# Layer 0's mixer in a fixed order by phase, with its closing norm kept in PSUM and its first state written by ScalarE

## The chip, the cores and the metric

The kernel runs on one core of a Trainium2 chip. The metric is device time in microseconds (us) of one execution; the number of record is the median of several runs. Five engines work side by side, each through its own queue in program order: PE (TensorE, matrix products; PEld is its loading of weights), DVE (VectorE), ACT (ScalarE), POOL (GpSimd) and SP (here only the issuing of transfers). They wait for each other by semaphores. Matrix products land in PSUM, which has eight banks of 128 x 512 fp32; everything else lies in SBUF.

## The reference, cut to what matters

The whole program is four layers on an image of 4 x 32 x 128 x 128 fp32. Only layer 0 is touched. For each of the four images (`b`), with 32 time steps of 128 nodes x 128 features, it computes a group norm, a graph attention with a layer norm after it, and then a selective state-space mixer (Mamba) over the 32 time steps, whose result is normed and added to the input:

```python
xz = xt @ in_proj                       # xc (256 wide) and the gate z (256 wide)
xc = silu(conv over 4 time steps of xc)
dbc = xc @ x_proj                       # dt's input, B (16), C (16)
dt = softplus(dbc[..., :8] @ dt_w + dt_b)
def step(hprev, inp):                   # for each of 32 time steps
    dA_t, dBx_t, C_t = inp              # dA = exp(-dt*exp(A_log)), dBx = dt*xc*B
    hnew = dA_t * hprev + dBx_t         # state: 128 nodes x 256 channels x 16
    return hnew, einsum('bds,bs->bd', hnew, C_t)
y = (ys + Dp * xc) * silu(z)
out = y @ out_w + out_b                 # then h + out, layer norm (gain nt_g, bias nt_b), x + that
```

## The kernel before

`layer0` (a function of class `Kernel`) goes through the four images. Each image has two stages: `gat`, the attention, in 8 groups of 4 time steps; and `mamba`, the mixer, in 8 blocks of 4 time steps. Both write no instruction directly. They register **parts** (an engine, a cost in us, a function that issues some instructions, what it comes after, which buffers it takes and frees) with a planner, class `Parts`; `emit` then orders all parts by a list schedule: of the parts that could start, it takes the one that starts first by the costs, ties within a `patience` going to the lower **rank** (a number per kind, `RANKS`, plus the part's place in time). Every engine then executes its instructions in just the order of emission (`in_order`). The costs, the stretch factors and the ranks are thus all that decides the order in each queue.

What a mixer block does, by the names that the prediction uses:

- `mamba_block` prepares a block while the block before it runs: `conv` (8 matmuls of 512 columns into two banks), `xsilu` (ACT, Silu), `xproj`, `dbc`, `dtproj`, then softplus by `dabs`, `dexp`, `one`, `dln` (Ln), `back` on ACT, `relu` on DVE and `dplus` (L1060) and `dsub` (L1063) on POOL, which ends in `dt`; `xturn` and `umul` (L1074, DVE) make `u` = dt x xc, `bct` and `bc` (L1085) B and C.
- `mamba_gates` makes silu(z): two matmuls (`gatep`) into two banks, then both banks by ACT (`zsilu`).
- `step` does one time step in four quarters of four states each. Per quarter: `decay` (POOL, L755) makes dt x A into `e` (three buffers); `expo` (ACT, L761) puts exp(-e) into a PSUM pair `pa` (two such pairs); `mul` (DVE, L775) multiplies by the state `S` in place; `plus` (DVE, L783, four instructions) adds u x B and writes `S`. For the fourth quarter ACT makes u x B (`ub`, L791) and one DVE sum adds it (L795). The first time step has no old state: DVE writes u x B straight into `S` (L785, 16 instructions from SBUF to SBUF). `diagp` (POOL, L772) and `diag` (ACT, L767) make diagonals of C, and `read` (PE, L808) contracts S with them into the PSUM tile `yp`; `fetch` (ACT, L816) copies that out, `turn` (PE, L821, L826) turns it and adds Dp x xc, and `gate` (DVE, L834) multiplies by silu(z).
- `output` closes the block: `project` (PE, L876 to L882, one part) into a bank of the pool `pm`; `ofetch` (ACT, L888) copies the bank to SBUF, which frees it; `stats` (DVE, L895, L897), `power` (POOL, L901 to L904), `norm` (ACT, L909) and `sums` (POOL, L913, L914, L916: times gain, plus bias, plus X).

PSUM is divided into `pa` (four banks), `yp` (two) and `pm` (two banks, for everything else; a part that takes a `pm` bank has to come after the one that frees it). ACT holds one table of functions at a time; a change among Exp, Silu and Ln puts a table load in front. When block 6 is registered (`HEAD`), parts of the next image's attention are registered too, named `ahead`: `gat_open` makes its coefficients (DVE L398 to L403, then PE's spread L407, then ACT's copy L411), and `gat_inputs` the inputs of its first two groups. The rank `EARLIER` puts them late in the order. The last block's close of images 0 to 2 is left to the next image's `gat`.

## Time and profile before

| what | us |
|---|---|
| runs of the kernel, median (lowest to highest of 3) | 3815.86 (3815.35 to 3816.46) |
| the profiled execution, its own time | 3811.59 |
| its span, from the first to the last instruction | 3809.8 |
| mean granted TensorE clock | 0.88 |
| layer 0 | 0 to about 2283 |
| the mixers, from first decay (L755) to last read-out (L816) | 162 to 595, 723 to 1158, 1286 to 1718, 1844 to 2267 |
| the three attention stages between them | 128, 128, 126 |

Busy shares over the span are PE 82%, DVE 77%, ACT 70%, POOL 66%; but they are a mean over four layers with different limits, and POOL has little to do after layer 0. The page's line of POOL in 40 slices shows this:

```profile
POOL 3699896699996799896799980133456522067940
```

Each digit is a slice of 95 us, 9 for 90% and more. The four runs of 8 and 9 up to slice 24 are the four mixers. The profile's groups name an instruction by its line in the kernel, its engine, and what it writes and reads; "idle before" is the time that its engine stood still just ahead of it, with the instruction that ended this.

### The profile page before, as it was taken

The page shows a single profiled execution, that of the slowest core. Times are in us where ns is not written, and L with a number is a line of the kernel's source. Part 1 is how long each engine was busy: PE and PEld are TensorE (multiplying, and loading weights), DVE is VectorE, ACT ScalarE, POOL GpSimd, SP SyncE. Part 2 cuts the span into 40 slices and gives each one's busy share as a digit, 9 for nine tenths or more (in the row PEclk, how much of TensorE's full clock was granted, in tenths as well). Part 3 has the DMA queues.
Part 4 walks back from the last instruction along what each step waited for, and adds up shares of the span by engine and source line. Part 5 has one row for each costly group of instructions (what it writes and reads, how often), then busy time and mean ns, then how long its engine had stood idle before and what let it go on. Part 6 is the DMA issues. An engine that isn't in the chain of part 4 may idle for free. (4 is left out here: it accounts for less than half of the span.)

```text
span 3809.8 us, 64520 instructions
## 1 busy us (share of the span) xinstructions
PE 3133.8 (82%) x23495; PEld 2082.4 (55%) x23495; DVE 2938.7 (77%) x6986; ACT 2676.5 (70%) x5577; POOL 2525.0 (66%) x2043
## 2 busy tenths in 40 slices
PE   7888888888878888778888868787868987988877
PEld 4555455455545454455445447665547753587655
DVE  6788997898997898897789875577869856386942
ACT  5799896789896888886899873334566654176753
POOL 3699896699996799896799980133456522067940
PEclk8888899988999988899888885797869998998989
DMA  3000000000000000000000000000002000700003
GB/s 127 1 1 1 1 1 1 1 1 1 1 1 1 1 1 1 1 1 1 1 1 1 1 12 7 1 1 1 1 18 81 1 1 3 267 4 1 1 1 89
DMA packets 51654, 61.38 MB, mean 16 GB/s; under 512 B 5850, under 2 KB 31140, under 8 KB 51204
## 3 DMA queue, kind: packets, MB, share of 16 engines
q1 hardware_dynamic: 36740, 42.12, 3.3%
q10 hardware_dynamic: 14592, 15.08, 1.1%
q8 instruction: 188, 3.08, 0.3%
q14 instruction: 134, 1.10, 0.1%
HBM read 48.80 MB, written 8.39 MB: 15 GB/s over the span
## 5 line engine op out<-in xcount | busy, mean ns | idle before, releaser
L755 POOL TENSOR_TENSOR e<-dt,Ar 128x1024 f32<-128x1024 f32 x496 | 1180.1, 2412 | 33.4 <-ACT pa L761 32.2
L775 DVE TENSOR_TENSOR pa<-pa,S 128x1024 f32<-128x1024 f32 x496 | 607.0, 1224 | 49.6 <-ACT pa L761 48.7
L783 DVE SCALAR_TENSOR_TENSOR S<-u,BC,pa 128x256 f32<-128x256 f32 x1488 | 615.3, 475 | 22.8 <-DVE pa L775 1.4
L761 ACT ACTIVATE pa<-e 128x1024 f32<-128x1024 f32 x496 | 502.7, 1019 | 83.1 <-DVE S L783 37.6
L808 PE MATMUL yp<-S,Dp 64*64 64x256 f32 x4096 | 359.0, 504 | 122.3 <-issue 57.4
L808 PE MATMUL yp<-S,D 64*64 64x256 f32 x4096 | 293.9, 397 | 93.3 <-DVE S L795 69.7
L808 PEld LDWEIGHTS yp<-S,Dp 64*64 64x64 f32 x4096 | 192.8, 175 | 274.2 <-issue 155.9
L767 ACT ACTIVATE D<-I,BC 128x64 f32<-128x64 f32 x1024 | 262.5, 337 | 0.1
L808 PEld LDWEIGHTS yp<-S,D 64*64 64x64 f32 x4096 | 155.5, 138 | 185.4 <-issue 63.0
L1006 PE MATMUL pm<-h,Wm 128*128 128x512 f32 x512 | 237.0, 612 | 0.0
L826 PE MATMUL pm<-I,y 128*128 128x64 f32 x1024 | 171.9, 299 | 55.9 <-ACT y L816 55.9
L791 ACT ACTIVATE ub<-u,BC 128x256 f32<-128x256 f32 x496 | 210.1, 495 | 9.6 <-DVE S L795 6.8
L559 POOL TENSOR_TENSOR e<-e,den 128x512 f32<-128x512 f32 x128 | 131.7, 1041 | 118.6 <-DVE den L555 69.3
L772 POOL TENSOR_TENSOR Dp<-I,BC 128x256 f32<-128x256 f32 x256 | 156.2, 626 | 78.9 <-PE yp L808 70.5
L826 PEld LDWEIGHTS pm<-I,y 128*128 128x128 f32 x1024 | 162.1, 226 | 63.8 <-ACT y L816 63.8
L547 ACT ACTIVATE e<-sc,mn 128x128 f32<-128x128 f32 x512 | 145.9, 400 | 31.9 <-DVE mn L542 19.1
L1006 PEld LDWEIGHTS pm<-h,Wm 128*128 128x128 f32 x512 | 95.7, 194 | 116.4 <-issue 115.7
L795 DVE TENSOR_TENSOR S<-pa,ub 128x1024 f32<-128x1024 f32 x124 | 151.6, 1222 | 6.0
L821 PE MATMUL pm<-xc,DD 128*128 128x128 f32 x512 | 129.0, 338 | 5.3 <-DVE dt L1045 5.3
L542 DVE TENSOR_REDUCE mn<-sc 128x4 f32<-128x512 f32 x128 | 83.0, 680 | 57.3 <-PE sc L533 41.4
L821 PEld LDWEIGHTS pm<-xc,DD 128*128 128x128 f32 x512 | 88.8, 217 | 48.2 <-issue 37.1
L761 ACT ACT_TABLE_LOAD x88 | 112.9, 1283 | 1.5
(599 smaller groups left out, 8093.1 us busy)
## 6 DMA issues: line engine op xcount, KB each, us to landing
w<-in_L_ffn_weight_dram SPq DMA_DIRECT2D x22, 1024.0 KB, 14.7
w<-in_L_ffn_weight_dram ACTq DMA_DIRECT2D x10, 1024.0 KB, 13.7
out_dram<-o ACTq DMA_DIRECT2D x16, 256.0 KB, 2.9
out_dram<-o SPq DMA_DIRECT2D x16, 256.0 KB, 2.9
X<-in_x_dram SPq DMA_DIRECT2D x4, 512.0 KB, 5.6
A<-in_L_conv_A_log_dram SPq DMA_DIRECT2D x1, 2048.0 KB
cw<-in_L_conv_conv_w_dram SPq DMA_DIRECT2D x1, 512.0 KB
sh<-in_sh_dram SPq DMA_DIRECT2D x1, 512.0 KB, 3.7
```

Source lines behind the costliest of these rows:

```text
L755: nc.gpsimd.tensor_tensor(v["e", q], node("dt").unsqueeze(1).to_broadcast([P, 4, 256]), Ar[:, 4 * q : 4 * q + 4, :], ALU.mult)
L761: nc.scalar.activation(v["a", q], v.pop(("e", q)), AF.Exp, scale=-1.0)
L767: nc.scalar.activation(v["D", q][:, r, :], I2, AF.Copy, scale=g["BC"][:, i, s : s + 1])
L772: nc.gpsimd.tensor_tensor(v["D", q], I2.unsqueeze(1).to_broadcast([P, 4, 64]), C, ALU.mult)
L775: nc.vector.tensor_tensor(v["a", q], v["a", q], S[:, 4 * q : 4 * q + 4, :], ALU.mult)
L783: nc.vector.scalar_tensor_tensor(S[:, s, :], node("u"), Bt, a[:, r, :], ALU.mult, ALU.add)
L791: nc.scalar.activation(v["b", q][:, r, :], node("u"), AF.Copy, scale=g["BC"][:, i, s : s + 1])
L795: nc.vector.tensor_tensor(S4, v.pop(("a", q)), v.pop(("b", q)), ALU.add)
L808: nc.tensor.matmul(v["y"][o : o + 64, n, :256], D[ns, r, :], S[ns, s, :], start=(s < 2), stop=(s >= 14), skip_group_check=True,)
L821: nc.tensor.matmul(v["p"][:, j * P : (j + 1) * P], DD[:, j, :], g["xc"][:, j, cs], start=True, stop=False)
L826: nc.tensor.matmul(v["p"][:, o : o + 64], v["y"][:, n, j * P : (j + 1) * P], I2, start=False, stop=(n == 1))
L1006: nc.tensor.matmul(g["x", j], Wm[:, i, j * P : (j + 1) * P], rows(4 * k + 3 - i), start=(i == 0), stop=(i == 3))
```

## The change

The mixer's planner no longer makes a list schedule. Each part gets the rank `block x PERIOD + phase`, where `PERIOD` is 52.093 and `PHASES` holds one phase for each part of a block by its kind, and `emit` issues the parts in order of rank, each as soon as all that it comes after has been issued. All blocks have so the same order. The parts `ahead` have ranks of block 0 to 3. Beside this:

- `output`: `project` in four parts; no `ofetch`; `stats` and `norm` work on the bank itself; the product with the gain (`gain`) is DVE's, in the bank; the bias is added to X by POOL (`shift`), at any time before; `total` (DVE) adds bank and X. The bank is held until `total`. Where the next image's attention closes the last block (images 0 to 2), the copy and the three sums stay.
- `plus` of the first time step is 16 ACT copies with a scale instead of 16 DVE instructions.
- `mamba_gates` and `mamba_block` take one bank at a time for each half (`zsilu`, `xsilu`), and `conv` is eight parts of one matmul.
- Costs of most kinds, the stretch factors and the ranks of `gat` (still list-scheduled, with an added 0.13 us between dependent parts of one engine) have new values.

The diff, cut to its core (new values of costs and of the tables left out):

```diff
+    def emit(self):
+        if self.by_rank:
+            left = sorted(self.parts, key=lambda p: p["rank"])
+            while left:
+                p = left.pop(next(i for i, p in enumerate(left) if self.start(p) is not None))
+                for h in p["take"]:
+                    self.taken[h["name"]].append(h)
+                p["end"] = 0.0
+                p["fn"]()
+            return
...
-        plan = Parts(latency=0.25, window=300, patience=self.PATIENCE, stretch=Parts.STRETCH)
-        hold, pace = plan.hold, 25.5
-        def add(kind, at, *args, **kwargs):
-            plan.rank = at * pace + self.RANKS[kind]
+        plan = Parts()
+        plan.by_rank, seen = True, {}
+        hold = plan.hold
+        def add(kind, k, *args, **kwargs):
+            n = seen[kind, k] = seen.get((kind, k), -1) + 1
+            plan.rank = k * self.PERIOD + self.PHASES[kind][n]
             return plan.add(*args, **kwargs)
...
-                        nc.vector.tensor_scalar(S[:, s, :], node("u"), Bt, None, ALU.mult)
+                        nc.scalar.activation(S[:, s, :], node("u"), AF.Copy, scale=Bt)
...
+            def take():
+                g["x"] = g.pop("p").rearrange("p (a f) -> p a f", f=F)
+                stats()
+            def shift():
+                nc.gpsimd.tensor_tensor(xs, xs, ntb.unsqueeze(1).to_broadcast([P, 4, P]), ALU.add)
+            def gain():
+                nc.vector.tensor_tensor(g["x"], g["x"], ntg.unsqueeze(1).to_broadcast([P, 4, P]), ALU.mult)
+            def total():
+                nc.vector.tensor_tensor(xs, g["x"], xs, ALU.add)
...
-            p = add("project", 4 * k + 4, PE, 3.4, project, g["gates"], [hx, hp], [g["h"]["yg"]])
-            p = add("ofetch", 4 * k + 4, ACT, 0.52, fetch, [p], (), [hp])
+            for i in range(4):
+                p = add(
+                    "project", k, PE, 1.6 if i == 0 else 0.78, lambda i=i: project(i), [p] if i else g["gates"],
+                    () if i else [hp], [g["h"]["yg"]],
+                )
...
+                p = add("stats", k, DVE, 1.06, take, [p])
+                p = add("power", k, POOL, 1.78, power, [p])
+                p = add("norm", k, ACT, 1.54, norm, [p])
+                p = add("gain", k, DVE, 0.6, gain, [p])
+                x = add("shift", k, POOL, 1.23, shift)
+                add("total", k, DVE, 0.6, total, [p, x], (), [hp])
...
                 def ahead(kind, at, *args, **kwargs):
-                    plan.rank = self.EARLIER * pace + at
-                    return plan.add(*args, **kwargs)
+                    return add("ahead", 0, *args, **kwargs)
...
-        hs, c = [hold("pm", 2), hold("pm", 2)], None
+        c, p = None, None
         for j in range(2):
-            c = add("gatep", 4 * k, PE, 0.92, lambda j=j: gatep(j), [c], () if j else [h["sz"], *hs])
-        g["sz ready"] = [add("zsilu", 4 * k, ACT, 1.0, both, [c], (), hs, "silu")]
+            hp = hold("pm", 2)
+            c = add("gatep", k, PE, 0.965, lambda j=j: gatep(j), [c], [hp] if j else [h["sz"], hp])
+            p = add("zsilu", k, ACT, 0.49, lambda j=j: zsilu(j), [c, p], (), [hp], "silu")
+        g["sz ready"] = [p]
```

In the order of the changed program's instructions (it has no times in it) a block runs on POOL with one `shift` and no `sums`, on DVE from `stats` to `total` as: stats, L783's four, L775, L783's four, L775, `gain`, L795, `total`, and on PE from `project` to the first matmul of conv's second half as: six quarters of `read` with conv's first four matmuls between them. The coefficients of the next image stand on DVE ahead of the stage's first L775, and the `ahead` copy of ACT ahead of the last four copies of the first state. The program has 142 table loads, 60 fewer than before; 58 POOL instructions fewer and 58 DVE products more; 64 DVE scalings fewer and 64 ACT copies more; 29 ACT bank copies fewer.

## The prediction

> **What bounds the kernel now.** I read the busy time by stage first, then the groups, then who waited for whom inside a stage, then single stretches of the timeline. Layer 0 handles four images in turn; each has an attention stage (some 128 us) and a mixer stage (some 430 us). Busy time of PE, PEld, DVE, ACT and POOL in the second image's mixer, the third's attention and the fourth's mixer, then clock and DMA:
>
> ```profile
> 723.00:1158.00 435.00, 355.37 (x2945) 215.40 (x2944) 395.42 (x668) 378.44 (x694) 398.99 (x245) 0.87 0.00 1
> 1158.00:1286.00 128.00, 109.22 (x990) 68.56 (x982) 90.13 (x233) 92.38 (x237) 79.54 (x97) 0.97 0.01 1
> 1844.00:2267.00 423.00, 349.69 (x2913) 213.71 (x2914) 377.20 (x658) 377.11 (x696) 393.47 (x242) 0.86 0.00 1
> ```
>
> In a mixer stage POOL is busy 399 of 435 us, DVE 395, ACT 378: POOL leads, two others are close behind. The big groups (out<-in, count, busy, mean ns):
>
> ```profile
> L755 POOL TENSOR_TENSOR e<-dt,Ar 128x1024 f32<-128x1024 f32 x496 | 1180.1, 2412 | 33.4 <-ACT pa L761 32.2
> L775 DVE TENSOR_TENSOR pa<-pa,S 128x1024 f32<-128x1024 f32 x496 | 607.0, 1224 | 49.6 <-ACT pa L761 48.7
> L783 DVE SCALAR_TENSOR_TENSOR S<-u,BC,pa 128x256 f32<-128x256 f32 x1488 | 615.3, 475 | 22.8 <-DVE pa L775 1.4
> L761 ACT ACT_TABLE_LOAD x88 | 112.9, 1283 | 1.5
> ```
>
> Durations overlap a little, so I price by starts of neighbours. POOL's timeline in a mixer, and the end of a block in it:
>
> ```profile
> 788.16 14.23 POOL L755 TENSOR_TENSOR e<-dt,Ar 128x1024 f32<-128x1024 f32 x6
> ...
> 817.21 1.21 POOL L772 TENSOR_TENSOR Dp<-I,BC 128x256 f32<-128x256 f32 x2
> 818.35 2.37 POOL L1060 TENSOR_TENSOR dt<-dt,u 128x1024 f32<-128x1024 f32 x1
> 820.80 2.36 POOL L1063 TENSOR_TENSOR dt<-dt,u 128x1024 f32<-128x1024 f32 x1
> 823.24 2.39 POOL L755 TENSOR_TENSOR e<-dt,Ar 128x1024 f32<-128x1024 f32 x1
> ```
>
> ```profile
> 516.14 1.30 POOL L913 TENSOR_TENSOR xn<-xn,ntg 128x512 f32<-128x512 f32 x1
> 517.51 1.28 POOL L914 TENSOR_TENSOR xn<-xn,ntb 128x512 f32<-128x512 f32 x1
> 518.87 1.27 POOL L916 TENSOR_TENSOR X<-X,xn 128x512 f32<-128x512 f32 x1
> 520.10 2.39 POOL L755 TENSOR_TENSOR e<-dt,Ar 128x1024 f32<-128x1024 f32 x1
> ```
>
> One block of the mixer on POOL: 16 decays of 14.23/6 = 2.37 make 37.9; four pairs of diagonals of 1.14 (817.21 to 818.35) 4.6; dplus and dsub 4.9 (818.35 to 823.24); the norm's power step 1.8 (L901 at 808.34 to the next decay at 810.12); the three sums 4.0 (516.14 to 520.10). Together 53.1 us. By POOL's timeline the blocks 1 to 7 of the last image begin 55.1 us apart on average (1883.7 to 2214.3, six periods), those of the second 55.9 (770.1 to 1105.6). So POOL is idle 2.0 us a block, 2.8 where the next image's inputs are opened in the same stage. **A mixer block is POOL's own work plus two to three us.**
>
> Two stretches show something else. DVE builds the first state (L785), then next image's coefficients (L398), while POOL runs:
>
> ```profile
> 720.42 16.97 DVE L785 TENSOR_SCALAR S<-u,BC 128x256 f32<-128x256 f32 x16
> ```
>
> ```profile
> 429.07 9.32 POOL L755 TENSOR_TENSOR e<-dt,Ar 128x1024 f32<-128x1024 f32 x4
> ...
> 431.31 7.10 DVE L398 TENSOR_TENSOR gc<-gd 128x1 f32<-128x1 f32 x1
> ```
>
> L785 takes 0.34 us where POOL rests and up to 2.5 us beside a decay; 16 of them fill 17.0 us. L398, a 128x1 product, ends at 438.41, just as POOL's four decays end (438.39). The same line takes 0.16 us at 19.9 us, where POOL has little to do. Both read SBUF alone; DVE's other large groups read a bank as well and show no such stretch.
>
> **The change, part by part.**
>
> *Closing norm in its bank.* For 29 of 32 blocks POOL's three sums become one (shift): -2 x 1.35 = -2.7 us, so 53.1 becomes 50.4. DVE gains two products of 128x512 with one side in a bank. Nearest rows: half of L775's 1.13 us between starts, and L591 (0.58 to 0.62); I take 0.6 each, +1.2. ACT loses the copy L888 (0.48). DVE's block by starts: 16 x 1.13 (L775) + 12 quarters x 4 x 0.39 (L783) + 4 x 1.13 (L795) + 3.9 (gates, relu, umul, BC) + stats 1.04 + 1.2 = 47.6, plus 0.13 for each L775 whose own L783 follows at once (median of its starts 1.26 against 1.13), some 1.2: 48.8. Still under POOL's 50.4. The trace of before has no stats or norm on a bank that is also the matmul's target; bounds: stats between 0.19 (L596, SBUF) and 0.17 a quarter (0.69/4, L355 from a bank), so nothing either way.
>
> [...]
>
> *Tables.* The changed program holds 142 table loads where before has 202. 60 x 1.29 us (start to next start) = 78 us less on ACT, about 2.4 a block. ACT is not the bound, so this is worth nothing alone; it is the cover for the first state, and it shortens the wait of L775 on ACT (48.7 us in all).
>
> *First state by ACT.* 64 L785 leave DVE (14.9, 17.0, 15.0 and 9.3 us in the four stages) and 64 copies of 128x256 come to ACT, 0.40 each by L791: 6.4 us a stage.
>
> *Ahead.* The next image's coefficients move from the middle of the stage (block 4) to its head. In before they come with a POOL idle of 2.8 - 2.0 = 0.8 us a block, 4.8 us a stage, in three stages; that goes. But in the changed order the product that was L398 stands behind POOL's power of the next image, and POOL has 2 decays and 3 diagonals (2 x 2.37 + 3 x 0.57 = 6.5 us) right behind that. I take the full 6.5 us, by the 7.10 row. Behind it on DVE stand the diagonals; behind these, PE's spread, which holds the first reads; behind the spread ACT's copy of the row, and behind that the last quarter of the first state, a diagonal, a table load and the first exponential: 15.8 us after dsub for the row (dsub, powers and the first decay 7.5, stall 6.5, diagonals and PE 1.8), +1.6 +1.0 +1.3 +1.0 = 20.7 to the first L775. Before it is 21.3, 22.4 and 20.5 (dsub's end 714.9 to 737.3). So the head gains nothing in three stages; in the fourth, without that product, 14.3 against 14.0.
>
> [...]
>
> *Order by phases.* Every block follows one fixed order instead of a list made by due times. After the first exponential ACT has, in the new order, 12 exponentials (0.95), two diagonals or inputs between most of them, four table loads and the next block's chain: 40 us to block 1, against 36.4 from the first L775 now: +3 a stage. The next block's conv to dsub stands at fixed places, and POOL's last decay of a block comes well before dplus, so POOL must wait when that chain is late. I keep the idle at 2.0 a block: 50.4 + 2.0 = 52.4. Bounds: 1.0 (the waits of POOL on PE, 18.4 us of the second mixer, mostly gone) and 4.0 (twice). The last block: 52.8 us from its first decay to its last read-out; fewer sums, but POOL now ahead of DVE: -1.
>
> *Gates by bank, conv in single matmuls, project in four:* the same instructions on PE and ACT, in smaller parts. PE is busy 355 of 435 us and hides them: nothing; without that cover a late bank costs what the held-bank rival below prices. *Attention ranks:* two table loads fewer (2.6 us of ACT beside PE's 109 of 128), other order unknown, bounds -5 and +5: I take -2 a stage.
>
> **Sum.** Mixers of images 1 to 3: 6 x (55.9 - 52.4) = 21, +1, -3 = 19 each, 57. Fourth: 6 x (55.1 - 52.4) = 16, +1, -3 = 14. Attention 4 x 2 = 8. End of the layer, where the sums are bare: copy 0.5 and 2.7 gone, 3. Total 82. The profiled execution took 3811.59 us (span 3809.8); less 82, 3729.6. The median of the runs is 3815.86, 4.3 above: **3734 us**.
>
> **Rivals.**
>
> *DVE becomes the bound.* 48.8 plus its waits: in the second mixer 32 us (13.5 on umul's bank, 11.4 on ACT, 4.9 on gates, others 2.2), 4 a block; 48.8 + 4.0 = 52.8, and with somewhat more in a fixed order 53.7: 28 blocks x 1.3 = 36, **3770**. For it: DVE gains 1.2 a block where POOL loses. Against: table loads caused part of the waits.
>
> *More than forecast.* No stall at the head (-5 x 3), idle of 1.5 (-0.5 x 28): **3705**; with attention at -5, 3693.
>
> *The held bank stalls PE: slower.* A project bank was free after 0.6 us of copy; now it is held through stats, power, norm, gain and total, one of two. In the new order PE has 6 quarters of reads (1.09 each by L808's 16 records) and 4 conv matmuls (0.93 each) before conv's second half wants that bank: 10.2 us. DVE's order from stats to total is 1.0 + 5.4 + 0.6 + 1.1 + 0.6 = 8.8 if power (1.8) and norm (1.5) return within the 5.4. They have 1.8 us to spare there and 1.4 at PE; a decay (2.4) ahead of power and an input group (1.6) ahead of norm eat 4.0. Beyond 3.2 us, conv is late, then dplus, and POOL idles by as much. At 4 us a block: 28 x 4 = 112, **3846**; it decides from 82/28 = 2.9 us a block. Against: only both queues at their worst give 0.8.
>
> *Nothing to be seen:* a fixed order loses just what POOL saves, 3816. That the change does not do what it says I rule out: its program has 58 fewer POOL instructions and 60 fewer loads.
>
> **Chances.** Forecast 0.45 (own range 3710 to 3755), DVE 0.25, more 0.15, held bank 0.12, nothing 0.03. Faster by over 0.2% 0.85, within 0.2% (about what a measurement can tell from no change) 0.03, slower 0.12. With the bounds of idle (1.0: -28; 4.0: +56) and attention (-12, +28) the range is 3680 to 3800.
>
> **What would show it.** Blocks 1 to 7 begin 52.4 us apart on POOL; shift once a block; the old L398 takes some 6 us in three stages, and POOL idles at the head for it; mixer stages of 413 to 416 us, the fourth 409; L775's wait on ACT below 40. Wrong if POOL's idle per block is above 3, if conv waits for total, or if DVE's waits fall on gain.

## The result, and the profile after

| | before | changed |
|---|---|---|
| runs: median (lowest to highest), us | 3815.98 (3815.34 to 3819.27, 6 runs) | 3842.05 (3829.98 to 3862.76, 6 runs) |
| ratio, 95% interval | | 1.0072 (1.0045 to 1.0099) |
| profiled execution, span | 3809.8 | 3837.3 |
| mean granted clock | 0.880 | 0.881 |

The change made the kernel 0.7% slower; 3734 was forecast. The stages of the changed kernel, second image's mixer, third's attention, fourth's mixer (columns as in the prediction: busy us of PE, PEld, DVE, ACT, POOL, then the granted clock):

```profile
718.60:1170.10 451.50, 372.21 (x2950) 226.42 (x2950) 384.51 (x672) 365.60 (x696) 389.70 (x242) 0.85 0.00 1
1170.10:1294.90 124.80, 106.30 (x978) 67.31 (x978) 87.72 (x224) 87.27 (x229) 71.79 (x86) 0.97 0.01 1
1859.20:2295.40 436.20, 362.44 (x2915) 218.61 (x2916) 375.29 (x663) 363.59 (x692) 385.34 (x238) 0.86 0.00 1
```

POOL, DVE and ACT each have 9 to 13 us less to do in the second mixer, and the stage is 16.5 us longer: all three have less work and more idle time. The page's groups say where the engines stand idle (last columns: idle time ahead of the group, and what ended it); the changed kernel's, and before's row of the read-out:

```profile
L818 POOL TENSOR_TENSOR e<-dt,Ar 128x1024 f32<-128x1024 f32 x496 | 1190.2, 2424 | 51.9 <-ACT pa L824 49.5
L838 DVE TENSOR_TENSOR pa<-pa,S 128x1024 f32<-128x1024 f32 x496 | 605.0, 1225 | 123.3 <-ACT pa L824 120.2
...
L1094 PE MATMUL pm<-h,Wm 128*128 128x512 f32 x512 | 251.1, 620 | 16.7 <-DVE X L991 16.7
...
L879 ACT COPY y<-yp 128x512 f32<-128x512 f32 x128 | 73.7, 576 | 139.1 <-PE yp L871 139.1
```

```profile
L816 ACT COPY y<-yp 128x512 f32<-128x512 f32 x128 | 73.0, 571 | 40.8 <-PE yp L808 40.8
```

DVE's wait for the exponential (L838) rose from 48.7 to 120.2 us. PE's wait in conv for `total` (L991), on which the held-bank rival rested, is 16.7 us in 32 blocks: that rival did not happen. ACT stands 139 us at the read-out (L879), where in before it stood 41 (L816), and what it waits for is PE.

A block's end, where the prediction saw POOL run on without a pause, on POOL, PE and ACT (a sub-block, here and in the expectations, is one of the block's four time steps):

```profile
308.49 0.69 POOL L835 TENSOR_TENSOR Dp<-I,BC 128x256 f32<-128x256 f32 x1
310.49 2.35 POOL L1148 TENSOR_TENSOR dt<-dt,u 128x1024 f32<-128x1024 f32 x1 [1.30 <-ACT u L1142]
314.72 2.37 POOL L1151 TENSOR_TENSOR dt<-dt,u 128x1024 f32<-128x1024 f32 x1 [1.89 <-ACT u L1145]
```

```profile
310.04 0.56 PE L889 MATMUL pm<-I,y 128*128 128x64 f32 x4
315.15 1.98 PE L871 MATMUL yp<-S,Dp 64*64 64x256 f32 x16 [4.55 <-issue]
...
320.66 1.99 PE L871 MATMUL yp<-S,Dp 64*64 64x256 f32 x16
...
324.18 3.41 PE L871 MATMUL yp<-S,D 64*64 64x256 f32 x32
```

```profile
314.48 0.56 ACT L879 COPY y<-yp 128x512 f32<-128x512 f32 x1
...
327.67 0.58 ACT L879 COPY y<-yp 128x512 f32<-128x512 f32 x1 [7.02 <-PE yp L871]
```

Three things are to be seen. POOL waits for the logarithm (L1142) and for the copy back (L1145). PE has nothing for 4.55 us ahead of the fourth sub-block's first reads, which start just as ACT has fetched the bank (314.48 and 0.56 us; the profile itself names no releaser). And after that gap a quarter of reads takes 1.98 us, where the prediction counted 1.09 by other such rows: PE runs at half speed, and the trace's clock records have half (0.50 granted) from 313.5 to 327.2 us. ACT stands 7 us for those reads, and the exponentials behind it, and with these DVE and POOL, come late.

Where the 27.5 us of the two spans lie, from POOL's and ACT's timelines (head: first decay of a mixer to that of its block 1; end: block 7's first decay to the last read-out; sums over four images):

| us | before | changed | difference | forecast |
|---|---|---|---|---|
| heads | 175.5 | 203.2 | +27.7 | +12 |
| 24 periods of blocks 1 to 7 | 1338.5 | 1334.4 | -4.1 | -79 |
| last blocks | 209.7 | 227.1 | +17.4 | -4 |
| attention stages, end of the layer | | | -15.1 | -11 |
| the other three layers | | | +1.6 | 0 |

### The profile page after: what moved, and what is told of

Its sections match the earlier page's. It is cut to its first block, busy times and chain, and to the rows that moved or that the text cites. A ratio compares the mean times of both kernels' runs of the same rounds, so it can differ in the third digit from the quotient of the medians.

```text
span 3837.3 us, 64436 instructions
## 1 busy us (share of the span) xinstructions
PE 3159.9 (82%) x23495; PEld 2099.7 (55%) x23495; DVE 2898.1 (76%) x6980; ACT 2605.5 (68%) x5552; POOL 2454.3 (64%) x1985
## 3 DMA queue, kind: packets, MB, share of 16 engines
q14 instruction: 134, 1.09, 0.1%
## 5 line engine op out<-in xcount | busy, mean ns | idle before, releaser
L838 DVE TENSOR_TENSOR pa<-pa,S 128x1024 f32<-128x1024 f32 x496 | 605.0, 1225 | 123.3 <-ACT pa L824 120.2
L871 PE MATMUL yp<-S,Dp 64*64 64x256 f32 x4096 | 348.0, 462 | 216.6 <-issue 106.2
L871 PEld LDWEIGHTS yp<-S,Dp 64*64 64x64 f32 x4096 | 181.3, 156 | 339.1 <-issue 151.3
L871 PE MATMUL yp<-S,D 64*64 64x256 f32 x4096 | 303.5, 425 | 17.5 <-ACT D L830 12.4
L1094 PE MATMUL pm<-h,Wm 128*128 128x512 f32 x512 | 251.1, 620 | 16.7 <-DVE X L991 16.7
L871 PEld LDWEIGHTS yp<-S,D 64*64 64x64 f32 x4096 | 183.8, 150 | 141.5 <-issue 54.1
L879 ACT COPY y<-yp 128x512 f32<-128x512 f32 x128 | 73.7, 576 | 139.1 <-PE yp L871 139.1
## 6 DMA issues: line engine op xcount, KB each, us to landing
w<-in_L_ffn_weight_dram SPq DMA_DIRECT2D x22, 1024.0 KB, 14.2
```

The source lines that it names most:

```text
L838: nc.vector.tensor_tensor(v["a", q], v["a", q], S[:, 4 * q : 4 * q + 4, :], ALU.mult)
L871: nc.tensor.matmul(v["y"][o : o + 64, n, :256], D[ns, r, :], S[ns, s, :], start=(s < 2), stop=(s >= 14), skip_group_check=True,)
L1094: nc.tensor.matmul(g["x", j], Wm[:, q, j * P : (j + 1) * P], rows(4 * k + 3 - q), start=(q == 0), stop=(q == 3))
```

## The experiments

Theory A, formed from these lines: in the fixed order POOL waits for ACT (copy back), and ACT for the read-out; the head is DVE's coefficients beside POOL. Its rival: the held bank. The theory that stood at the end, **P**, came out of the sixth run: PE's gaps let the granted clock fall (mean 0.881 in the changed kernel, 0.904 in e9, where two of them are filled), and the chain behind them runs at half speed (a quarter of reads in 1.98 us, 1.09 at full clock). Diffs are against the changed kernel, if no other is named; before was run beside all of them (3812.98 to 3818.46 median).

**e1: the copy back earlier.**

```diff
-        back=(-12.84,),
+        back=(-14.1,),
```

> The changed kernel with one phase moved: ACT's back stands before the block's second-to-last exponential and its table load, not behind them. In the changed profile POOL waits 1.9 us in each block at dsub for it (L1145). Theory A (the period is one loop: dsub, umul, last reads, the read-out on ACT, then ACT's queue in its fixed order until back, then dsub again): the period falls by most of 1.9 us and the time by 30 to 50 us against the changed kernel (3842), to about 3800. Theory B (the held bank stalls PE at conv) and theory C (DVE, with 49 us of work a block, is the bound): POOL's wait moves elsewhere, the time stays within 10 us of 3842.

3816.03 us, ratio 1.0009 (0.9984 to 1.0033): 26 us less. POOL no longer waits for the copy. But the periods are of two kinds: 52.9, 53.1, 57.7, 52.9, 53.4, 53.4 in the first image, 53.6 to 58.2 in the second, with the same instructions in the same order.

**e2: ACT goes to the last read-out of a block later**, so that exponentials pass it.

```diff
-        fetch=(13.41, 25.08, 39.36, 52.72),
+        fetch=(13.41, 25.08, 39.36, 53.6),
```

> The changed kernel with one phase moved: the read-out of a block's last step (L879) stands on ACT behind the next block's second exponential and its input group, not ahead of them. In the changed profile ACT stands still up to 7.0 us in a block for this read-out. Theory A: ACT does 2.6 us of work in that wait, the period falls by up to 2.4 us, the time by 40 to 65 us against the changed kernel, to about 3790. Theories B and C: within 10 us of 3842, because turn, gate and project come later by as much.

3879.66, 1.0162 (1.0144 to 1.018): 38 us more, the reverse of what was expected. Turn, gate, projection and the norm's statistics come later; POOL's power step then waits 2.1 to 3.3 us a block for them. Filling ACT's stand gains nothing, as what stands behind the read-out is on the path. The mean clock is lower too, 0.863, so not all of the 38 us need be the order's.

**e3: the next image's coefficients by ACT.**

```diff
-            nc.vector.tensor_tensor(c[:, 0:1], d[0][:, 2:3], d[0][:, 2:3], ALU.add)
-            nc.vector.scalar_tensor_tensor(c[:, 1:2], d[0][:, 0:1], -1.0, c[:, 0:1], ALU.mult, ALU.mult)
-            nc.vector.tensor_tensor(c[:, 1:2], c[:, 1:2], bo, ALU.add)
+            nc.scalar.activation(c[:, 0:1], d[0][:, 2:3], AF.Copy, scale=2.0)
+            nc.scalar.activation(c[:, 2:3], d[0][:, 2:3], AF.Copy, scale=-2.0)
+            nc.scalar.activation(c[:, 1:2], d[0][:, 0:1], AF.Identity, scale=c[:, 2:3], bias=bo)
...
-                nc.vector.tensor_scalar(s["D"][:, i, :], self.ident, c[:, i : i + 1], None, ALU.mult)
+                nc.scalar.activation(s["D"][:, i, :], self.ident, AF.Copy, scale=c[:, i : i + 1])
...
-        p = add("diag", 0, DVE, 1.2, diags, after)
+        p = add("diag", 0, ACT, 1.2, diags, after)
...
-        ahead=(-20.9, -132.51, 3.61,
+        ahead=(3.5, -132.51, 3.61,
```

> The changed kernel with the next image's coefficients (three small products and two diagonals) computed by ACT instead of DVE, at the same place in the head of the stage. In the changed profile DVE needs 6.4 us for them beside POOL's decays and POOL then waits 6.8 us for the first exponential. If the two engines lock each other out, the first exponential comes 4 to 5 us earlier in three stages: 12 to 15 us less than 3842. If the head is bound by ACT's own queue (first state, tables): no change or 3 us more.

3833.94, 1.005 (1.0033 to 1.0067): 8 us less, where 12 to 15 were expected. The head is 48.1 instead of 53.2 us in three stages, so 5.1 us each is DVE beside POOL; the 24 periods of blocks 1 to 7 are 6 us longer. In the changed kernel's third mixer:

```profile
1297.89 0.56 DVE L411 TENSOR_TENSOR gc<-gd 128x1 f32<-128x1 f32 x1 [3.55 <-POOL gd L395]
1298.49 2.26 DVE L412 SCALAR_TENSOR_TENSOR gc<-gd,gc 128x1 f32<-128x1 f32 x1
1300.78 0.53 DVE L413 TENSOR_TENSOR gc<-gc,bo 128x1 f32<-128x1 f32 x1
1301.24 3.01 DVE L416 TENSOR_SCALAR hg<-ident,gc 128x128 f32<-128x128 f32 x2
```

```profile
1303.55 0.61 POOL L835 TENSOR_TENSOR Dp<-I,BC 128x256 f32<-128x256 f32 x1
1310.92 2.42 POOL L818 TENSOR_TENSOR e<-dt,Ar 128x1024 f32<-128x1024 f32 x1 [6.75 <-ACT pa L824]
```

Five small instructions take 6.4 us from 1297.89, beside POOL's decays; POOL then waits 6.75 us for the first exponential, which stands behind them. It is DVE alone that is seen to be slow there: L412 takes 2.26 us, and 0.16 at 19.1 us, where POOL has little to do; the two decays beside the five take 2.34 us each, the median of all decays being 2.42.

**e4: the closing norm in its bank alone, in the kernel before** (list schedule; ranks of the five parts -1500):

```diff
-            p = add("ofetch", 4 * k + 4, ACT, 0.52, fetch, [p], (), [hp])
...
+                p = add("stats", 4 * k + 4, DVE, 1.45, take, [p])
+                p = add("power", 4 * k + 4, POOL, 1.8, power, [p])
+                p = add("norm", 4 * k + 4, ACT, 1.54, norm, [p])
+                p = add("gain", 4 * k + 4, DVE, 0.6, gain, [p])
+                x = add("shift", 4 * k + 4, POOL, 1.23, shift)
+                add("total", 4 * k + 4, DVE, 0.6, total, [p, x], (), [hp])
```

> The kernel before with one part of the change alone: the closing norm in its bank (stats, norm, gain and total there, one POOL sum a block instead of three, no copy), under the old list schedule. Where the fixed order is what loses (theory A), POOL's 2.7 us a block are saved here: 28 blocks make 60 to 80 us less than 3816, about 3745. Where the held bank (B) or DVE's two more products (C) lose it, it stays at 3810 to 3850.

3931.56, 1.029 (1.0273 to 1.0307), periods 51 to 71 us. POOL waits 5.3 to 7.3 us a block ahead of its diagonals (L772), longer for DVE's copy of B and C (113 of 187 us in all) than for PE's reads (72). The list schedule orders everything anew, so this prices the norm in the bank under that schedule, not the held bank alone.

**e5: e1 and e3 together.**

> The changed kernel with the two moves together that gained when made alone: back ahead of the second-to-last exponential (26 us less alone) and the next image's coefficients by ACT (8 us less alone). If they act on different places (each block's end, three heads), they add: 3842 - 34 = about 3808. If one loop carries both, less than 26 remains.

3815.88, 1.0004 (0.9989 to 1.0019), single runs from 3803.2 to 3831.7. The head keeps its gain; the periods still go from 52.5 to 58.1 us in one and the same order. Something outside the order decides.

**e6: conv with one of its four taps** (this leaves three quarters of the convolution out, 6 matmuls of 0.9 us a block).

```diff
-            nc.tensor.matmul(
-                g["x", j], Wm[:, q, j * P : (j + 1) * P], rows(4 * k + 3 - q), start=(q == 0), stop=(q == 3)
-            )
+            if q == 0:
+                nc.tensor.matmul(g["x", j], Wm[:, q, j * P : (j + 1) * P], rows(4 * k + 3 - q), start=True, stop=True)
```

> The changed kernel in which conv does one of its four taps: 6 of the 8 conv matmuls of a block are left out (5.6 us of PE a block, 32 blocks), so its result is not the reference's; order, banks and waits stay. Theory P (PE's own chain at a block's end, read-out, turn, gate, project, next reads, sets the period, and the stretches in which its clock is granted at half speed lengthen it): the blocks fall to 52 to 53 us, evenly, 50 to 80 us less than 3842. Theory C (DVE is the bound with 49 us a block) or the order of ACT's queue alone: the blocks stay at 54 to 57, less than 20 us change.

3849.54, 1.0082 (1.0061 to 1.0103). With 5.5 us less PE work a block (6 x 0.91, at full clock) nothing was won, and the mean clock fell:

```profile
core 0: 3853.4 us, clock 0.859
```

The changed kernel has 0.881. The clock records of the trace change only in steps of 3.41 us, between full and half (117 records each in the changed kernel); half lay on 18.3 us of a block here, on 12.6 in the changed kernel. In the mixers a step down follows a step in which PE was busy 0.52 of the time on average in the changed kernel, 0.37 in before; where the clock stays up the step before had 0.88 and 0.92. These are means: in the changed kernel the steps ahead of a step down go from 0.00 to 0.95 busy, so no threshold comes out of them. In e5 the 6 periods with under 7 us of half clock take 53.0 us on average, the 9 with over 12 us 57.3. So less PE work meant more half clock here. That is theory P.

**e7: the fixed order, but the norm with its copy and POOL's three sums**, as before.

```diff
-                p = add("stats", k, DVE, 1.06, take, [p])
+                p = add("ofetch", k, ACT, 0.485, fetch, [p], [hx], [hp])
+                p = add("stats", k, DVE, 1.06, stats, [p])
...
-                p = add("gain", k, DVE, 0.6, gain, [p])
-                x = add("shift", k, POOL, 1.23, shift)
-                add("total", k, DVE, 0.6, total, [p, x], (), [hp])
+                for i in range(3):
+                    p = add("sums", k, POOL, 1.23, lambda i=i: sums(i), [p], free=[hx] if i == 2 else [])
```

> The changed kernel with the close as before (copy of project's bank to SBUF by ACT, three sums by POOL), in the fixed order. POOL has 2.7 us more a block, DVE 1.2 less, the bank is free some 8 us earlier. If the held bank is what costs the changed kernel its gain (theory B): 3842 or less in spite of the longer POOL block. If the period is POOL's work plus the waits of the fixed order on ACT and PE (some 4.6 to 6.5 a block), it grows by up to 2.7 a block: 3880 to 3920.

3846.0, 1.0101 (1.0072 to 1.013): 2.7 us more of POOL work a block by the prediction's price cost 4 us in the whole program. POOL's idle time took it up (1.8 to 4.0 us a block instead of 4.4 to 6.2).

**e8: the first state by ACT alone, in the kernel before.**

```diff
-                        nc.vector.tensor_scalar(S[:, s, :], node("u"), Bt, None, ALU.mult)
+                        nc.scalar.activation(S[:, s, :], node("u"), AF.Copy, scale=Bt)
```

> The kernel before with one part alone: the first time step's state by ACT instead of DVE, list schedule. If DVE's 9 to 17 us beside POOL set the head of the stage, the first L775 comes 5 to 8 us earlier in three stages: 15 to 25 us less than 3816. If ACT's queue sets it (6.4 us of copies ahead of the first exponential), as I found for the changed kernel: within 5 us of 3816.

3851.38, 1.0091 (1.0073 to 1.011). The first product comes 6.5 us after the first decay instead of some 12, but the head stays at 45.0, and other periods of the list grow to 69. Inconclusive on its worth in the fixed order.

**e9: matmuls that nobody reads, in PE's gaps.**

```diff
+                for _ in range(5 if i == 1 else 0):
+                    nc.tensor.matmul(v["p"][:, 256:], self.ones, inp[:, 256:], start=True, stop=True)
                 for j in range(2):
...
-            nc.tensor.matmul(
-                g["x", j], Wm[:, q, j * P : (j + 1) * P], rows(4 * k + 3 - q), start=(q == 0), stop=(q == 3)
-            )
+            for c in (0, 1) if (j, q) == (0, 1) else (q,):
+                nc.tensor.matmul(
+                    g["x", j], Wm[:, c, j * P : (j + 1) * P], rows(4 * k + 3 - c), start=(c == 0), stop=(c == 3 or (j, q) == (0, 0))
+                )
```

> The changed kernel with matmuls that nobody reads in TensorE's two idle stretches of each block: five of 128x256 in the unused half of the second sub-block's turn bank (ahead of the 3.0 to 4.6 us gap before the fourth sub-block's reads), and the first tap of the first convolution twice (0.9 us, ahead of the 1.9 to 2.4 us gap before the second sub-block's reads). No wait, order or buffer of the work itself changes; nothing of the computation is left out. Theory P (the blocks lose their time because the granted clock goes to half after these gaps, and the chain of reads, turn, gate and projection then runs at half speed): the mean granted clock rises from 0.881 to 0.90 or more, the periods of 57 to 58 us go to 53 to 55, and the time falls by 20 to 50 us, to 3790 to 3825. Rival L (the chain is late because ACT reads the bank out late; the clock only follows): the periods stay at 54 to 58 or grow by the added 3.3 us of TensorE work, and the time is 3840 to 3900 whatever the clock does.

**3775.31, 0.9883 (0.9866 to 0.9899): 67 us less than the changed kernel, by adding 3.3 us of useless PE work to each block.** That is more than P asked for (20 to 50). The changed kernel's mean clock, this run's, and the same block end on PE, ACT and POOL (the five matmuls are ten records):

```profile
core 0: 3837.3 us, clock 0.881
```

```profile
core 0: 3773.1 us, clock 0.904
```

```profile
304.87 2.43 PE L884 MATMUL pm<-inp,ones 128*128 128x256 f32 x10
...
310.97 1.09 PE L871 MATMUL yp<-S,Dp 64*64 64x256 f32 x16 [2.39 <-issue]
...
313.92 1.09 PE L871 MATMUL yp<-S,Dp 64*64 64x256 f32 x16
...
315.89 1.96 PE L871 MATMUL yp<-S,D 64*64 64x256 f32 x32
```

```profile
317.92 0.58 ACT L879 COPY y<-yp 128x512 f32<-128x512 f32 x1 [1.44 <-PE yp L871]
```

```profile
306.31 2.36 POOL L1151 TENSOR_TENSOR dt<-dt,u 128x1024 f32<-128x1024 f32 x1
310.55 2.38 POOL L1154 TENSOR_TENSOR dt<-dt,u 128x1024 f32<-128x1024 f32 x1 [1.87 <-ACT u L1148]
```

The gap is 2.39 us instead of 4.55, the reads behind it take 1.09 instead of 1.98, ACT waits 1.44 instead of 7.02, and the clock records have full speed from 272.2 to 354.1 us. POOL keeps only the wait for the copy back. The periods are 52.6 to 53.3 nearly everywhere; half clock lies on 5.7 us of a block. The heads stay as long as in the changed kernel.

**e10: the gaps closed by order instead** (e5's kernel; two read-outs earlier on ACT).

```diff
-        fetch=(13.41, 25.08, 39.36, 52.72),
+        fetch=(13.04, 25.08, 38.0, 52.72),
```

> The kernel of the fifth run (copy back before the reads, coefficients by ACT) with two phases changed: the first sub-block's read-out of the bank moves ahead of the closing norm (13.41 to 13.04), the third's ahead of the exponential's table load (39.36 to 38.0). Rival L (ACT's order makes the reads late): the gap before the fourth sub-block's reads shrinks by the exponential and its table load, 2.3 us, the one before the second's by the norm's 1.7 us; up to 2 us a block, 3765 to 3800. Theory P gives the same sign, as the gaps shrink, and asks besides that the clock rises to 0.89 or more and that the blocks which keep a full clock are the short ones. Nothing (3805 to 3825) if the reads were not on the path.

3846.67, 1.0074 (1.0057 to 1.009), a miss: 31 us worse than e5. ACT now stands 5.2 to 6.0 us a block at the read-outs, the closing norm comes later, and conv's second half waits for `total` (L991) 65.7 us in all, where it was 16.7: here the held bank does bite.

**e11: e5 with e9's unread matmuls.**

> The kernel of the fifth run (copy back first, coefficients by ACT) with the unread matmuls of the ninth. Theory P: with the clock kept, the two edits give what they could not give in the fifth run. In the ninth run POOL is idle 2.15 to 3.2 us a block, 1.9 of it waiting for the copy back; without that wait a block comes to POOL's 50.4 plus some 0.3 to 1, so 50.7 to 51.5 instead of 52.6 to 53.3 in 24 periods (-29 to -45), and the head is 5 us shorter in three stages (-15): 3715 to 3745. Rival: another chain (ACT's read-out, the closing norm) holds the block at 52.6 as well, and only the head's 15 us are had: 3755 to 3765.

3752.86, 0.9837 (0.9824 to 0.985): the best version, 1.6% under before, its runs within 7.3 us. But 8 us short of what was expected, and nearer to the rival. The wait for the copy back is gone and two others have its place; one block on POOL:

```profile
299.82 2.37 POOL L1151 TENSOR_TENSOR dt<-dt,u 128x1024 f32<-128x1024 f32 x1 [1.33 <-ACT u L1145]
302.26 2.37 POOL L1154 TENSOR_TENSOR dt<-dt,u 128x1024 f32<-128x1024 f32 x1
...
324.70 0.24 POOL L970 TENSOR_SCALAR mrs<-mmv 128x4 f32<-128x4 f32 x1 [1.59 <-DVE mmv L966]
```

POOL's idle is 2.1 to 3.0 us a block, as in e9. The periods stay at 52.5.

**e12: unread matmuls in the kernel before**, in its own gaps (order unchanged).

```diff
-            nc.tensor.matmul(
-                g["z", j], inp[:, 256 + j * P : 256 + (j + 1) * P], h1[:, 4 * k + 3 : 4 * k + 7, :], start=True, stop=True
-            )
+            for _ in range(4 if j else 1):
+                nc.tensor.matmul(
+                    g["z", j], inp[:, 256 + j * P : 256 + (j + 1) * P], h1[:, 4 * k + 3 : 4 * k + 7, :], start=True, stop=True
+                )
...
+                for _ in range(2 if i == 3 else 0):
+                    nc.tensor.matmul(v["p"][:, 256:], self.ones, inp[:, 256:], start=True, stop=True)
```

> The kernel before with unread matmuls in its own two idle stretches of TensorE: the second gate matmul of each block four times (2.6 us, in the 3.3 to 4.9 us gap behind it), two of 128x256 ahead of the fourth sub-block's turn (1.0 us, in a gap of 1.6 us). The order of all engines is that of before. Theory P holds for any order of this mixer: the kernel before has 8 to 20 us a block at half clock as well, its clock rises by 0.01 to 0.02 and its time falls by 20 to 60 us, to 3755 to 3795. If the clock cost only the fixed order (whose blocks are tighter), nothing: 3808 to 3825. The difference to the ninth run (3775) is what the change is worth with the clock kept in both.

3760.24, 0.9858 (0.9843 to 0.9874). P holds for the other order too: the mean clock is 0.913, in before 0.880. With the clock kept in both, the change is still 15 us slower (3775.31 against 3760.24).

**e13: e7 with e9's unread matmuls.**

> The seventh run's kernel (fixed order, closing norm with the copy and the three POOL sums as before, so 2.7 us more of POOL work a block) with the unread matmuls of the ninth. If POOL is what bounds a block once the clock is kept (the prediction's rule: POOL's work plus a constant idle time), a block comes to 53.1 plus 1 to 2, that is 54 to 55 instead of 52.6, and the time to 3775 plus 24 times 1.5 to 2.5, 3810 to 3835. Rival (the fixed order, not POOL, sets 52.6; POOL's idle time takes the work up): 52.6 to 53.5 a block and 3775 to 3790.

3819.15, 1.0013 (1.0004 to 1.0022): 44 us more than e9, where e7 was 4 above the changed kernel. With the clock kept (0.901, in e7 0.881) POOL's work counts: 53.0 us of it, 1.4 to 1.9 idle, periods of 54.7 on average, where e9 has 50.6 and 53.1. Of the 2.4 us of added work a block 1.6 show in the period.

**e14: the same number of unread matmuls where no long gap follows** (first sub-block's turn, second convolution; diff against e9).

```diff
-                for _ in range(5 if i == 1 else 0):
+                for _ in range(5 if i == 0 else 0):
...
-            for c in (0, 1) if (j, q) == (0, 1) else (q,):
+            for c in (0, 1) if (j, q) == (1, 1) else (q,):
```

> The changed kernel with the same unread matmuls as in the ninth run, but where TensorE has no long gap behind them: the five of 128x256 ahead of the first sub-block's turn instead of the second's, and the first tap of the second convolution twice instead of the first's. Theory P (only work in the two gaps keeps the clock): the granted clock stays near 0.88, and the time stays at 3842 or rises by part of the 3.3 us a block, 3835 to 3900. Rival (any more TensorE work keeps the clock, or the later turn is what helped): the clock rises to 0.90 and the time falls to 3775 to 3800.

3896.9, 1.0209 (1.0195 to 1.0223): 55 us more than the changed kernel, at a mean clock of 0.888 and 11.9 us of half clock a block, hardly better than its 0.881 and 12.6. The place is what counts. The first mixer of e14, e9 and e12, in that order; the changed kernel's takes 438.5 us at 0.89:

```profile
157.20:612.50 455.30, 382.88 (x3044) 236.14 (x3044) 385.34 (x672) 366.93 (x696) 387.87 (x242) 0.89 0.00 1
```

```profile
154.60:578.50 423.90, 360.97 (x3045) 220.19 (x3045) 383.51 (x672) 366.80 (x697) 389.45 (x242) 0.93 0.00 1
```

```profile
157.10:576.80 419.70, 360.44 (x3022) 220.04 (x3021) 387.04 (x670) 376.97 (x695) 400.05 (x246) 0.94 0.00 1
```

**e18: e9's five matmuls behind the turn instead of ahead of it** (diff against e9).

```diff
-                for _ in range(5 if i == 1 else 0):
-                    nc.tensor.matmul(v["p"][:, 256:], self.ones, inp[:, 256:], start=True, stop=True)
                 for j in range(2):
...
+                for _ in range(5 if i == 1 else 0):
+                    nc.tensor.matmul(v["p"][:, 256:], self.ones, inp[:, 256:], start=True, stop=True)
```

> The ninth run's kernel with its five unread matmuls behind the second sub-block's turn instead of ahead of it, so that they start where TensorE's gap starts and make the turn no later; the first tap twice as there. Theory P (work in the gap keeps the clock): the same as in the ninth run, clock 0.90 and 3765 to 3785. Rival (the later turn, not the clock, is what helped there): 3820 to 3850.

3775.91, 0.9894 (0.9877 to 0.991), clock 0.901, as e9. So it was not the later turn that helped.

**e15: e11 with the first state on DVE**, as before the change.

```diff
-                        nc.scalar.activation(S[:, s, :], node("u"), AF.Copy, scale=Bt)
+                        nc.vector.tensor_scalar(S[:, s, :], node("u"), Bt, None, ALU.mult)
```

> The kernel of the eleventh run with the first state on DVE again, as before the change. The head (first decay to the next block's) is 46.3 us there, 40 us in the twelfth run (before with the clock kept). Theory H (the 16 first-state operations stand ahead of the first exponential on ACT's queue, 7 us of them after the first decay): the first multiplication comes 3 to 5 us sooner, the head is 41 to 43 us in the three stages, and the time falls by 8 to 15 us to 3738 to 3745. Rival (what holds the head is the next image's opening, its power on POOL behind a decay and its rows on ACT): the head stays at 45 to 48 and the time at 3750 to 3760.

3770.29, 0.9892 (0.9877 to 0.9907), a miss: the head is 49.7 instead of 46.3. The first state by ACT is a gain in this order, of 3.4 us in each of three stages and 6 in the fourth.

**e16: e11 with the next image's opening behind the first exponential.**

```diff
-        ahead=(3.5, -132.51, 3.61,
+        ahead=(6.5, -132.51, 9.35,
```

> The kernel of the eleventh run with the next image's opening behind the first exponential: its coefficients at phase 6.5 instead of 3.5, its row copy at 9.35 instead of 3.61; nothing else is moved. Theory O (the head is long because the first exponential stands behind the opening's coefficients and row copy on ACT, and these behind POOL's power): the first multiplication comes 4 to 5 us sooner (6.4 instead of 10.8 us after the first decay, as in the last image), the head goes from 46.3 to 42 to 43 us, the time falls by 8 to 14 us to 3739 to 3745. Rival (the head's end is held by something else): the first multiplication moves and the head stays at 46, 3750 to 3757.

3769.54, 0.9872 (0.9856 to 0.9887), a miss: 17 us more than e11. The first product comes 6.3 us after the first decay as expected, and the head is 50.7 us, longer than e11's. ACT's Silu of the next block now waits for conv:

```profile
736.67 0.69 ACT L1104 ACTIVATE xc<-pm,conv_b 128x512 f32<-128x512 f32 x1 [3.79 <-PE pm L1097]
```

**e17: e11 with logarithm and copy back ahead of an exponential.**

```diff
-        dln=(-14.15,),
+        dln=(-17.7,),
...
-        back=(-14.1,),
+        back=(-17.68,),
```

> The kernel of the eleventh run with the logarithm and the copy back ahead of the exponential of the fourth sub-block's third quarter (34.4 instead of 37.9 in the period). POOL waits 1.4 us a block for the logarithm and 0.9 for the closing norm there. If POOL still bounds the block, its wait for the logarithm goes and a block comes to 51.2 to 51.6: 3720 to 3735. Rival (DVE, which then waits for the exponential that comes 3.5 us later, takes over): 52.5 to 54, 3750 to 3790.

3908.74, 1.0239 (1.0225 to 1.0253), far outside both expectations: DVE's wait for the exponential goes from 127 to 234 us, periods to 56.6 to 61.2. The rival's mechanism, at four times its highest price (156 us over e11 instead of 37). But half clock is back as well, on 12.1 us of a block where e11 has 4.8; how much of the 156 us is which was not tried apart.

## Why the prediction was wrong

The stages with the clock kept, beside those without (sums over four images, us; half clock from the clock records, per period of blocks 1 to 7):

| | heads | 24 periods | last blocks | half clock |
|---|---|---|---|---|
| before | 175.5 | 1338.5 | 209.7 | 14.2 |
| changed | 203.2 | 1334.4 | 227.1 | 12.6 |
| e12: before, clock kept | 161.2 | 1302.0 | 206.5 | 5.3 |
| e9: changed, clock kept | 203.3 | 1274.0 | 215.4 | 5.7 |
| e11: e9 and two edits | 182.0 | 1269.9 | 220.8 | 4.8 |

- **The step that failed: "I keep the idle at 2.0 a block".** POOL's work came out as forecast (periods less their idle time are 50.5 us, 50.4 forecast); its idle was 4.4 to 6.2 (the images' means), over the upper bound of 4.0. The idle is no property of the block: it is how late the chain through PE and ACT comes, and half clock makes it late. Of the 75 us missing in the 24 periods, keeping the clock gives 60 back (1334.4 to 1274.0); the other 15 are 53.1 instead of 52.5 us a period. That the prediction read the clock column (0.86 and 0.87 in the mixers, 0.97 in attention) and made nothing of it was the blind spot: PE was called busy 355 of 435 us and therefore a cover, though that busy time was partly half speed.
- **The rule behind it was right under one condition.** "POOL's own work plus two to three us" holds in both fixed-order kernels once the clock is kept: 50.6 and 2.2 to 3.2 (e9), 53.0 and 1.4 to 1.9 (e13). POOL is not the only bound there: without its wait for the copy back (e11) the periods stay at 52.5. Without the clock POOL is not the bound and its saving is worth 4 us in all (e7).
- **And the saving is then small.** With the clock kept the 24 periods are 28 us shorter than before's (1302.0 to 1274.0), where 79 were forecast: before loses by half clock too (14.2 us a block). The forecast took what before would win as well for a gain of the change. And of the 28 us 26 lie in three periods, the block of images 1 to 3 in which before makes the next image's coefficients: in e12 it takes 61.6 to 62.1 us, L398 alone 7.6 to 8.9 beside POOL, and POOL is idle for 9.4 to 9.9; the fourth image, which opens none, has 53.2 there. That work moved into the head, where it costs again (5.1 a stage, e3). The other 21 periods are 53.2 us in e12 and 53.1 in e9, with POOL idle 0.4 and 2.5: what POOL saved there, the fixed order's waits took up, even with the clock kept. And POOL's saving is 2.1, not 2.7: before's periods less their idle time are 52.6, not the summed 53.1.
- **Head, forecast "gains nothing" and +3 a stage: wrong.** The stall beside POOL was set at 6.5 and is 6.4 us; but the first product comes 15.9 us after the first decay in three stages, in before 12.2 to 14.2. Counted from dsub's end, as the prediction counted, it comes after 27.9 to 28.3 us, where 20.7 was forecast and before has 20.5 to 22.4: the term "dsub, powers and the first decay 7.5" is 15.0 to 15.3 from there to the coefficients, as POOL also waits for attention's layer norm (4.46 us at L615 in the second image). From the first product to block 1 40 us were forecast against 36.4; the traces have 37.3 against 31.7 to 32.7, so before's had been put some 4 us too long and the loss is about 5, not 3. Taking the coefficients off DVE gives back 5.1 a stage (e3). With the clock kept in both, the heads lose 42 us (161.2 to 203.3), and 21 of these are still there in e11. Giving the first state back to DVE (e15) and moving the opening behind the first exponential (e16) both made the head longer; what holds the 21 us stays open.
- **Last block, forecast -1 each, was +4.4:** 11.7 of the 17.4 us are the clock (227.1 to 215.4), the rest is open.
- **Right:** DVE is busy 49.1 us a block (48.8 forecast) and is not the bound; attention and the layer's end took off 15.1 us (11 forecast), but partly by luck: 2 a stage were forecast for attention, and it was 7.3 in the first image, 2.6 and 2.8 in the next two, nothing in the fourth; the held bank stalled PE for 16.7 us in all, not 112. The time came out beside that rival's 3846, but not by its mechanism. The gates by bank and the new ranks of attention were not tried alone.
- **The range.** Its ends do not follow from the bounds it names: 3734 less 28 and 12 is 3694, and 3734 with 56 and 28 is 3818, not 3680 and 3800.

The 4.55 us gap above is one case of several: of the 71 steps down in the changed kernel's mixers 51 follow a 3.41 us step that no PE gap of over 3 us touches (those that e9 fills ahead of the fourth sub-block's reads are 3.0 to 4.6 us). The loss shows in the waits of the engines behind PE, as in ACT's 7.02 us above.

## What to carry to other kernels

Where engines wait for each other in a ring, look at the granted clock by stage and at one instruction's duration in two places (1.09 and 1.98 us here) before calling any engine a cover. Idle time of an engine did cost something here, as the clock went with it: a few unread matmuls exactly in the gap were worth 56 to 67 us (clock 0.880 to 0.913 in e12, 0.881 to 0.904 in e9), the same ones elsewhere cost 55 (e14, 0.888). An idle time taken over from one order into another was no constant here (2.0 us a block in before, 4.4 to 6.2 in the changed kernel); price it by what would make its last wait late.

## What the runs showed of the hardware

Less work was not faster: with 6 of 8 conv matmuls of a block left out, the granted clock fell from 0.881 to 0.859 and the time did not fall (e6). The changed kernel's runs spread over 33 us where before's spread over 4, and e11's over 7: in e5's ten runs the longer execution has the lower clock throughout (from 3803.2 us at 0.885 to 3831.7 at 0.875). A 128x1 scalar_tensor_tensor on DVE took 2.26 us beside a POOL decay of 2.34 (L412), while its neighbours L411 and L413 took 0.56 and 0.53.
